# Early gathers of a deformable convolution, staged through three tiles instead of three and then eight

## The chip, the cores and the metric

The kernel runs on one core of one Trainium2 chip. The metric is the device time of one execution in microseconds (us). The time before is the median of 12 runs.

## The reference, cut to what matters

Input `x` is (2, 256, 64, 64) in f32: two images (batches), 256 channels, 64 x 64 pixels. Four layers follow one another:

```
x = attention(x)                  # group norm, 4 heads, 4096 x 4096 scores per head, projection, residual
x = x + position_term             # a linear function of the pixel's place
x = bottleneck(x)                 # 1x1 to 64 channels, deformable 3x3, 1x1 back to 256, residual
h = relu(group_norm(x))           # 32 groups
h = deform_conv(h, dw1, pw1, w1)  # offsets from a 7x7 depthwise and a 1x1 convolution,
h = relu(group_norm(h))           # bilinear samples at 9 taps, 3x3 product
h = deform_conv(h, dw2, pw2, w2)
return h + x
```

A bilinear sample of one pixel and tap needs four neighbours of 256 channels each. The kernel keeps the image in DRAM (`img3`) such that one row of 1024 f32 values holds what a sample needs. A gather fetches 128 such rows, for 128 pixels and one tap: 512 KB. A block of 512 pixels takes 4 x 9 = 36 gathers.

## The kernel before

The kernel is one program written out in Python loops. Its first long stage is `attention`, its second is `deform`. The instructions of the matrix engine (PE), ScalarE (ACT), VectorE (DVE) and GpSimd (POOL) run in the order in which the Python code emits them: line 1666 asks for that with `manual_schedule`. The DMA queue of SyncE (SP) is not in that list. Its order is drawn up by the framework's own planner, and an SP instruction can be moved ahead of others that were emitted earlier. Each queue runs in order once the order is fixed: an instruction that waits holds up all that follow it.

**Attention.** It works through four units (two images, two pairs of heads). A unit is 256 steps `n`, and the main loop (line 677) takes two steps in each turn. Sixteen steps, eight turns, make a block of 256 queries: scores (L580), their maximum (L592), exponentials (L598), transposes (L610) with their copies (L627, L629), and the product with the values (L639). The accumulated product is copied into a tile `o` by DVE (L471), four times in a block. When the block's products are through, the following happens one after another:

- PE transposes the shares of the block, DVE copies them out (`shares`, L504), SP stores them to DRAM (`share_d`, L506) and loads them back spread over the partitions (`f`, L510);
- POOL multiplies `o` by `f` and adds it up (`combine`, lines 514 to 527, in the profile L519, L520, L525). Only then may DVE write the next block's product into `o`, since there is one buffer of `o`, of `f` and of `avs`;
- in every second block SP loads the residual (`res<-xa`, L214), and twelve steps into the block after that PE projects, and SP stores the result (`xa<-res`, L557). There is one buffer of `res` too.

In step numbers counted from a block's start: the shares of the block before are stored at step 0, its `combine` is emitted at step 4, its projection at steps 11 and 12.

**Background work.** Between these steps generators emit work of later layers (line 661). In the last unit these are the bottleneck's first half for image 1, and `early_samples` (line 1234), which the change touches. It computes the offsets for the first two blocks (`EARLY = 2`) of the first deformable convolution on image 0, and gathers their samples while attention still runs. Gathered rows go to DRAM (`samp_d`), since there is no room to keep them, and `deform` reads them back.

**The staging.** One gather goes through one 512 KB tile: POOL issues the indirect DMA from `img3` into the tile (L848), SP issues the store of the tile to `samp_d` (L1278), and then the tile may be gathered into again. `gather` (line 1273) does one store and one gather in each call:

```
if len(stores) > 1 and len(free) < 3 or not gathers and stores:
    dst, four = stores.popleft()
    nc.sync.dma_start(dst, four)
    free.append(four)
if gathers:
    dst, idx = gathers.popleft()
    four = free.popleft()
    self.gather(four, self.img3[0], idx)
    stores.append((dst, four))
```

The main loop makes one call a turn, and two in the turns of steps 10, 12 and 14 (line 726): 11 calls a block. At the start three tiles `xb` are free. When the offsets of the second block have been computed, five tiles that held their inputs join them (`whole`: two `v`, one `k`, two `bx`). From then on eight tiles go round.

A `combine` of POOL stands between the calls of the turn before it and that of its own turn, so 11 gathers lie between one `combine` and the next in POOL's order.

Of the kernel before, what the change touches and what calls it, by code (L numbers as in the profile page):

```python
# [29 lines left out]
EARLY = 2  # L30
# [34 lines left out]
class Net:  # L65
# [1168 lines left out]
    def early_samples(self, bott, pools, held, xp, vp, kp, ps):  # L1234


        nc, a = self.nc, self.a
        T, half = DWK * DWK, DWK // 2
        xs = [vp.tile([P, 8, P], F32, name="v").rearrange("p m c -> p (m c)") for _ in range(2)]
        src = self.xn_d[0].rearrange("(cb p) n -> p cb n", p=P)  # L1240

        def rows(i):
            return max(0, 8 * i - half), min(H, 8 * i + 8 + half)

        def load(i):
            y0, y1 = rows(i)
            for cb in range(2):
                nc.sync.dma_start(xs[cb][:, : (y1 - y0) * W], src[:, cb, y0 * W : y1 * W])


        xbs = [xp.tile([P, 2, 512], F32, name="xb") for _ in range(4)]
        held.append(xbs.pop())
        t = pools["t"].tile([P, 512], F32, name="bst")
        dw = t[:, : 2 * T].rearrange("p (c t) -> p c t", c=2)
        pw = t[:, 2 * T : 2 * T + 4 * K2].rearrange("p (c o) -> p c o", c=2)
        nc.sync.dma_start(dw, a["dw"][0])
        nc.sync.dma_start(pw, a["pw"][0])
        load(0)
        border = kp.tile([P, 2, 512], F32, name="k").rearrange("p u n -> p (u n)")
        wide = border[:, : 8 * (W + DWK - 1)].rearrange("p (r w) -> p r w", w=W + DWK - 1)  # L1260
        nc.gpsimd.memset(wide, 0.0)
        yield True
        wf, whole = [], xs + [border]
        for cb in range(2):
            t = pools["x"].tile([P, 2, 512], F32, name="bx").rearrange("p u n -> p (u n)")
            whole.append(t)
            wf.append(t[:, : T * 2 * K2].rearrange("p (t o) -> p t o", o=2 * K2))
            self.filters(wf[cb], cb, dw, pw)
            yield True
        free = deque(x.rearrange("p u n -> p (u n)") for x in xbs)  # L1270
        gathers, stores = deque(), deque()

        def gather():


            if len(stores) > 1 and len(free) < 3 or not gathers and stores:
                dst, four = stores.popleft()
                nc.sync.dma_start(dst, four)  # L1278
                free.append(four)
# [5 lines that stand above are left out]
            return gathers or stores  # L1285

        self.sample = gather
        for i in range(EARLY):
            idx = bott.corner.tile([P, 4, K2], I32, name="bidx")
            w = bott.corner.tile([P, 4, K2, 4], F32, name="bw4").rearrange("p a k c -> p (a k c)")  # L1290
            w = self.early[i] = w.rearrange("p (s j k t) -> p s j k t", s=2, j=4, t=2)
            steps = self.offsets(
                i, xs,
                lambda s, row: wf[s][:, DWK * row : DWK * row + DWK, :].rearrange(
                    "p t o -> p (t o)"
                ),
                self.vec[:, V_PWB : V_PWB + 1],
                bott.base, idx, None, pools["work"], wide, ps,
                odp=lambda: pools["t"].tile([P, 512], F32, name="bst"), y0=rows(i)[0],
                later=ps.later, w=w,  # L1300
            )
            mine = False
            for done in steps:
                if done == "bank":
                    continue
                while bott.lock and not mine:
                    yield False
                bott.lock = mine = True
                yield True
            bott.lock = False  # L1310
            if i + 1 < EARLY:
                load(i + 1)
            if i + 1 == EARLY:
                free.extend(whole)
            for m in range(4 * K2):
                k, j = divmod(m, 4)
                gathers.append((self.samp_d[i][m * P : m * P + P, :], idx[:, j, k : k + 1]))
# [443 lines left out]
```

## Time and profile before

| | |
|---|---|
| median of 12 runs | 5107.22 us (5102.15 to 5110.67) |
| the profiled execution | 5106.64 us, span 5104.8 us |
| PE busy | 4831.2 us, 95% of the span |
| DVE, ACT, POOL busy | 77%, 64%, 46% |
| DMA of `software_dynamic` (POOL's gathers) | 690.41 MB |
| DMA of `hardware_dynamic` (SP's queue) | 300.73 MB |
| gathers into the staging tiles | 32 into `xb`, 16 into `v`, 16 into `bx`, 8 into `k`: 72 |
| first and last of them, start | 2612.7 us and 2909.5 us |
| stores to `samp_d`, first and last issue | 2616.8 us and 2922.3 us |

A line of the timeline gives the start in us, the time in us, the engine and source line, the operation, the tiles written and read, a count, and in brackets the engine's idle time before it and what ended that. A line of the waits gives the engine and what it was about to do, what it waited for, the total in us, the number of times and the longest. A line of the windows gives, for one stretch, its length and then for each engine the busy us with the number of instructions, the granted PE clock, the busy share of the DMA engines and GB/s. Durations of PE are modelled, since matmuls are pipelined.

### The profile page before, as it was taken

How to read it: one execution, taken by the hardware profiler on the slowest of the kernel's cores; microseconds unless marked ns; L12 is line 12 of the kernel's file. 1: busy time of each engine (PE TensorE's matmuls, PEld its weight loads, DVE VectorE, ACT ScalarE, POOL GpSimd, SP SyncE). 2: the span in 40 equal slices, each digit the busy share in tenths (PEclk: the TensorE clock that was granted, in tenths of full speed). 3: DMA queues.
4: the chain of work that ended last, by engine and by line, in shares of the span. 5: the costliest groups of instructions: out<-in, count | busy, mean ns of one | idle time of the engine just before them, and what ended most of it. 6: DMA issues, size and time to landing. Idle time of an engine off the chain costs nothing. (4 is left out here: it accounts for less than half of the span.)

```text
span 5104.8 us, 101084 instructions
## 1 busy us (share of the span) xinstructions
PE 4831.2 (95%) x38680; PEld 2730.2 (53%) x38680; DVE 3948.4 (77%) x7033; ACT 3283.1 (64%) x5941; POOL 2331.1 (46%) x2256
## 2 busy tenths in 40 slices
PE   8999999999999999999999967779999999999998
PEld 5555565555566555565556534434544544444444
DVE  6878867878768888677667657667788888988888
ACT  5676656666667666666657643347876766666666
POOL 0111111111016777555112347775777676666665
PEclk9999999999999999999999979879999999999999
DMA  5131121111112333332547757669999999999998
GB/s 173 58 100 50 46 70 49 35 47 31 55 53 78 103 100 96 98 89 71 155 139 294 275 212 234 202 225 336 369 356 346 373 378 360 364 397 355 351 357 337
DMA packets 367028, 997.74 MB, mean 195 GB/s; under 512 B 61372, under 2 KB 98810, under 8 KB 366542
## 3 DMA queue, kind: packets, MB, share of 16 engines
q0 software_dynamic: 196560, 690.41, 37.2%
q1 hardware_dynamic: 169438, 300.73, 17.6%
q8 instruction: 304, 4.98, 0.4%
q14 instruction: 182, 1.49, 0.1%
q10 hardware_dynamic: 544, 0.13, 0.0%
HBM read 855.36 MB, written 127.35 MB: 193 GB/s over the span
## 5 line engine op out<-in xcount | busy, mean ns | idle before, releaser
L598 ACT ACTIVATE e<-sc,low 128x1024 f32<-128x1024 f32 x1024 | 1147.4, 1120 | 740.0 <-DVE low L592 737.3
L848 POOL DMA_INDIRECT four<-img,didx x1080 | 1153.6, 1068 | 531.6 <-issue 142.7
L592 DVE TENSOR_REDUCE low<-sc 128x1 f32<-128x1024 f32 x1024 | 1204.4, 1217 | 232.2 <-PE sc L580 227.8
L1545 PE MATMUL out<-st,wc 128*128 128x512 f32 x2304 | 1209.9, 608 | 72.3 <-ACT st L1535 34.0
L580 PE MATMUL sc<-k,qs 64*128 64x512 f32 x2048 | 998.0, 605 | 1.8 <-ACT e L598 1.4
L639 PE MATMUL av<-et,v 128*64 128x256 f32 x8192 | 998.2, 386 | 0.0
L580 PE MATMUL sc<-k,q 64*128 64x512 f32 x2048 | 977.2, 604 | 0.0
L519 POOL TENSOR_TENSOR o<-o,f 128x1024 f32<-128x1024 f32 x63 | 149.6, 2375 | 1766.9 <-DMA f<-share_d 883.8
L610 PEld LDWEIGHTS tt<-ident,e 64*128 64x128 f32 x16384 | 655.2, 139 | 513.0 <-issue 271.1
L629 ACT COPY et<-tt 128x512 f32<-128x512 f32 x1152 | 659.5, 585 | 173.4 <-PE tt L610 172.3
L610 PE MATMUL tt<-ident,e 64*128 64x64 f32 x16384 | 727.4, 226 | 36.1 <-ACT et L629 17.7
L627 DVE COPY et<-tt 128x512 f32<-128x512 f32 x896 | 611.6, 683 | 161.7 <-PE tt L610 161.3
L639 PEld LDWEIGHTS av<-et,v 128*64 128x64 f32 x8192 | 554.0, 137 | 301.7 <-issue 49.1
L848 POOL DMA_INDIRECT bfour<-img,bidx x576 | 587.6, 1020 | 183.9 <-issue 106.7
L1526 PEld LDWEIGHTS pt<-ident,smp 128*128 128x128 f32 x2304 | 328.3, 143 | 621.3 <-issue 479.2
L1495 DVE SCALAR_TENSOR_TENSOR four<-four,dwt 128x512 f32<-128x512 f32 x648 | 484.7, 748 | 220.5 <-ACT four L1489 218.8
L1514 DVE SCALAR_TENSOR_TENSOR smp<-four,dw,smp 128x256 f32<-128x256 f32 x1296 | 625.8, 483 | 33.8 <-ACT smp L1504 1.9
L1489 ACT ACTIVATE four<-four,dwt 128x512 f32<-128x512 f32 x648 | 466.2, 719 | 245.4 <-DMA four<-img,didx 241.6
L1545 PEld LDWEIGHTS out<-st,wc 128*128 128x128 f32 x2304 | 387.3, 194 | 319.3 <-issue 213.5
L580 PEld LDWEIGHTS sc<-k,qs 64*128 64x128 f32 x2048 | 346.3, 188 | 209.6 <-issue 116.5
L1526 PE MATMUL pt<-ident,smp 128*128 128x128 f32 x2304 | 445.1, 276 | 1.6 <-DVE smp L1508 1.1
L805 PE MATMUL pd<-x,wf 128*126 128x512 f32 x840 | 428.5, 592 | 0.0
(194 smaller groups left out, 4857.8 us busy)
## 6 DMA issues: line engine op xcount, KB each, us to landing
f<-share_d SPq DMA_DIRECT2D x128, 256.0 KB
four<-samp_d SPq DMA_DIRECT2D x64, 512.0 KB
xb<-xn SPq DMA_DIRECT2D x55, 512.0 KB
img<-imgt SPq DMA_DIRECT2D x96, 256.0 KB
four<-img,didx POOLq DMA_INDIRECT x1080
xa<-res SPq DMA_DIRECT2D x32, 512.0 KB
samp_d<-xb SPq DMA_DIRECT2D x32, 512.0 KB
xb<-in_x SPq DMA_DIRECT2D x20, 512.0 KB
```

The source lines that it names most:

```text
L580: nc.tensor.matmul(s[:, j, :], lhsT=q[u, i // 2][int(h != j)][halves[j], at : at + P], rhs=k[u][c][halves[j], h, :], start=True, stop=True,)
L592: nc.vector.tensor_reduce(low, s, AX.X, ALU.max, negate=True)
L598: nc.scalar.activation(e.rearrange("p j n -> p (j n)"), s, AF.Exp, bias=blk.low[:, g, c : c + 1], accum_out=blk.sum[:, g, c : c + 1],)
L610: nc.tensor.transpose(pt[:, m, :], e[half, m // 4, m % 4 * P : m % 4 * P + P], self.ident[half, half],)
L627: nc.vector.tensor_copy(dst, pt)
L629: nc.scalar.copy(dst, pt)
L639: nc.tensor.matmul(now["av"][halves[h], :], lhsT=v[u][c][:, m, halves[h]], rhs=ets[j][:, m, h, :], start=(m == 0), stop=(m == 7),)
L848: self.nc.gpsimd.indirect_dma_start(out=dst, out_offset=None, in_=img, in_offset=bass.IndirectOffsetOnAxis(ap=idx, axis=0),)
L1495: nc.vector.scalar_tensor_tensor(uv, four[:, 2 * C :], share(s, 1, 1), uv, ALU.mult, ALU.add)
L1514: nc.vector.scalar_tensor_tensor(smps[s], four[:, c], weight(s, c), smps[s], ALU.mult, ALU.add)
L1526: nc.tensor.transpose(pts[u][:, c, j * P : (j + 1) * P], smp[:, c * P : c * P + P], self.ident,)
L1545: nc.tensor.matmul(outs[ob], lhsT=wc[k][:, c, ob * P : ob * P + P], rhs=sts[u][:, c, :], start=(k == 0 and c == 0), stop=(k == K2 - 1 and ...
```

## The change

The five tiles no longer join. The list `whole` is gone, and so is the condition `len(free) < 3`, which made stores wait while tiles were plenty. Number, size and order of the gathers stay, and so do the 72 stores.

```diff
-        wf, whole = [], xs + [border]
+        wf = []
         for cb in range(2):
             t = pools["x"].tile([P, 2, 512], F32, name="bx").rearrange("p u n -> p (u n)")
-            whole.append(t)
             wf.append(t[:, : T * 2 * K2].rearrange("p (t o) -> p t o", o=2 * K2))
             self.filters(wf[cb], cb, dw, pw)
             yield True
...
-            if len(stores) > 1 and len(free) < 3 or not gathers and stores:
+            if len(stores) > 1 or not gathers and stores:
                 dst, four = stores.popleft()
                 nc.sync.dma_start(dst, four)
                 free.append(four)
...
             if i + 1 < EARLY:
                 load(i + 1)
-            if i + 1 == EARLY:
-                free.extend(whole)
             for m in range(4 * K2):
                 k, j = divmod(m, 4)
                 gathers.append((self.samp_d[i][m * P : m * P + P, :], idx[:, j, k : k + 1]))
```

## The prediction

> **What bounds the kernel now.** The page comes first, for where the time is and where the change acts.
>
> ```profile
> PE 4831.2 (95%) x38680; PEld 2730.2 (53%) x38680; DVE 3948.4 (77%) x7033; ACT 3283.1 (64%) x5941; POOL 2331.1 (46%) x2256
> ```
>
> PE is the bound on average, which says little about the 300 us in which the 72 staged gathers run (2612 to 2922 us). So next comes POOL's timeline over that stretch, which shows three tiles and eight tiles at work, one after the other:
>
> ```profile
> 2606.38 1.26 POOL L520 TENSOR_TENSOR o<-o 128x512 f32<-128x512 f32 x1
> 2607.72 0.72 POOL L525 TENSOR_TENSOR avs<-o 128x256 f32<-128x256 f32 x1
> 2612.65 0.98 POOL L848 DMA_INDIRECT xb<-img,bidx  x1 [4.21 <-DVE bidx L768]
> ...
> 2623.41 0.94 POOL L848 DMA_INDIRECT xb<-img,bidx  x1 [7.27 <-DMA samp_d<-xb]
> ...
> 2633.82 0.94 POOL L848 DMA_INDIRECT xb<-img,bidx  x1 [6.98 <-DMA samp_d<-xb]
> ...
> 2644.77 0.94 POOL L848 DMA_INDIRECT xb<-img,bidx  x1 [6.12 <-DMA samp_d<-xb]
> ...
> 2673.84 0.73 POOL L525 TENSOR_TENSOR avs<-o 128x256 f32<-128x256 f32 x1
> 2674.71 0.97 POOL L848 DMA_INDIRECT v<-img,bidx  x1
> ...
> 2693.00 0.94 POOL L848 DMA_INDIRECT k<-img,bidx  x1 [1.54 <-DMA samp_d<-k]
> 2714.33 2.35 POOL L519 TENSOR_TENSOR o<-o,f 128x1024 f32<-128x1024 f32 x1 [20.39 <-DMA f<-share_d]
> ...
> 2718.12 0.73 POOL L525 TENSOR_TENSOR avs<-o 128x256 f32<-128x256 f32 x1
> ```
>
> The first ten gathers use three `xb`. The 1st, 4th, 7th and 10th start at 2612.65, 2623.41, 2633.82 and 2644.77: a round of three costs 10.4 to 11.0 us, 10.7 on average, and each waits for the store of the tile. From 2674.71 on eight tiles serve, and the 11 gathers between two combines are issued within 18.3 us (to 2693.00). Then POOL idles 20.39 us for `f`. By this view alone the slack is large. SP's timeline of the same block says where `f` is held:
>
> ```profile
> 2702.07 0.32 SPq L1278 DMA_DIRECT2D samp_d<-v  x1
> 2704.55 0.32 SPq L1278 DMA_DIRECT2D samp_d<-k  x1
> 2704.97 0.38 SPq L506 DMA_DIRECT2D share_d<-shares  x1
> 2709.65 1.11 SPq L510 DMA_DIRECT2D f<-share_d  x2
> ```
>
> The store of the 11th gather stands ahead of `share_d` in SP's queue, although the code emits it later: the planner moved it there. `share_d` follows 0.42 us behind it, then `f`, then the combine. Two blocks later the order is the same, and the last store goes out at 2796.00 and `share_d` at 2796.41, while DVE had the shares ready at 2790.68 (2790.41 + 0.27). The waits between 2600 and 2930 us show the next link:
>
> ```profile
> POOL o L519 <- DMA f<-share_d: 107.0, 5, 25.2
> DVE o L471 <- POOL avs L525: 12.2, 5, 5.1
> ```
>
> DVE waits for the combine in five blocks, 5.1 us at the longest. So there is a closed loop: combine, 11 gathers, their stores, `share_d`, `f`, combine. It has no PE in it, and it sets or nearly sets the pace of these blocks. The windows between ends of combines show how near PE is:
>
> ```profile
> 2674.60:2718.90 44.30, 44.16 (x509) 27.48 (x504) 34.85 (x62) 31.64 (x62) 14.73 (x14) 1.00 0.72 274
> 2766.60:2810.10 43.50, 40.92 (x461) 24.82 (x460) 32.23 (x60) 28.34 (x55) 14.70 (x14) 1.00 0.74 279
> ```
>
> PE fills 94% to 100%. Loop and PE are balanced within a few us: whatever is added to the loop is not covered.
>
> **The change part by part.** It adds and removes no instruction and no byte. The condition without `len(free) < 3` does nothing by itself: with three tiles, two outstanding stores leave one free. What acts is that 62 gathers lose five of eight tiles; the first ten had only three before as well.
>
> One full block, from the end of a combine (T0): before, the last store goes out at T0 + 29.98 (2704.55 - 2674.57), + 29.64 and + 29.43 in the next two (2748.49 - 2718.85, 2796.00 - 2766.57): 29.7. After it, by the rows of the first block: the first gather at T0 + 0.1 (2674.71 - 2674.57); the 10th three rounds later, 32.1 us (2644.77 - 2612.65). The 11th follows the 10th as the 5th the 4th or the 8th the 7th, 1.25 or 2.65 us (2624.66 - 2623.41, 2636.47 - 2633.82): I take 2.0. Its store follows by 5.1 us, as that of the 10th did (issue over at 2650.16, so begun at 2649.84), or up to 6.1 as that of the second (2620.02 - 2613.94): 5.4. Sum: 0.1 + 32.1 + 2.0 + 5.4 = 39.6. The loop gets longer by 9.9 us, between 8.7 and 11.2.
>
> Behind it the path is as before: in the block above 9.4 us from `share_d` to the combine's start and 4.5 us of combine. The shares are ready at T0 + 24 to T0 + 30, so `share_d` goes on following the last store. While POOL waits for a tile, only gathers and the next combine are queued behind, and for that one DVE's copy of `o` waits, behind which stand the score maxima, the exponentials, and after a turn PE.
>
> Full blocks with 11 gathers on eight tiles: from 2674.57 to 2901.85 there are five (44.3, 47.7, 43.5, 48.4, 43.4 us). 5 x 9.9 = 49.5 us. The last block has seven gathers (10 + 55 + 7 = 72): its seventh store would go out at T0 + 0.1 + 21.2 + 4.3 = 25.6 instead of 20.4 (2922.30 - 2901.85). But `share_d` waits there for the residual's store and load anyway, until 2933.76. I take 2 of the 5 us. In two of the five blocks `xa<-res` and `res<-xa` stand between the last store and `share_d` (5.7 us, 2748.49 to 2754.16). If the planner now puts them ahead of the last stores, 2 x 4 to 5 us are saved: bounds 39 and 61 with the other terms' ends. I leave them where they are, at + 51.5.
>
> Sum: 5106.6 + 51.5 = 5158. The profiled run is 0.6 us under the median, so against that 5158 or 5159. Nothing is given back later: `deform` starts when attention ends, and its reads of `samp_d` are issued from 2974 us on, 50 us behind the last store.
>
> A rule that speaks against this loss: the Trainium skill, "DMA: Bandwidth & Descriptors", section "Anatomy of one DMA", gives a DMA's time as about 2.0 us and its bytes by 436 GB/s. For 512 KB that is an estimate of 3.2 us, 6.4 us for gather and store, 3 x 6.4 + 1.25 + 3.2 = 24 us for the last landing, earlier than now, and the sum would be nothing. The trace has 4.2 us from gather to store (2612.65 to 2616.84) and 6.6 from store to the next gather (to 2623.41), so the measured round stands.
>
> **The rivals.** *SP's queue gets another order, no change.* SP's order is the planner's. If the slower ring makes it place `share_d` ahead of the last two or three stores, `f` no longer waits for them. Then the 11th gather ends at T0 + 35, and the combine can start when it does now, T0 + 39.8. Cost 0 to 2 us a block: 5107 to 5117, say 5111. For it: 39.6 is later than the shares' 24 to 30. Against it: in the first block with three tiles, ten stores stand ahead of `xa<-res` and `share_d` in SP's order. It decides where `share_d` stands before the ninth store.
>
> *The same order, faster.* If `share_d` goes out as soon as the shares are there, up to 5.7 us earlier, the 12.2 us of DVE's waits could go: down to 5106.6 - 12.2 = 5094. Against it: the combine still has to follow the 11th gather at T0 + 35, and PE has 0.1 to 2.6 us of idle time a block in the windows shown.
>
> *Only PE counts.* In the first block with three tiles (2608 to 2674) the combine waited for DVE's `o`, not for `f`; the ring was hidden by 66 us of PE work. If blocks grow so, less is lost. In the later ones PE has 41 to 47 us, against a loop of 39.6 + 13.9 = 53.5 or more, so half the loss is the most that this may take away: 5118 to 5140.
>
> *More than summed.* Rounds of 12.5 us under the other traffic, or a lower clock after PE's new gaps (1.00 in most of these windows, 0.92 in the last): 5 x 6 us more, about 5190.
>
> **How the numbers follow.** The forecast, 5140 to 5172, gets 0.62; half the loss 0.10; more 0.07: slower 0.79. No change 0.14, faster 0.07. About 0.2% (10 us) is what a measurement of this kernel tells from no change. The range of 8 in 10 takes in the forecast, the half and the edges of its neighbours: 5111 to 5176.
>
> **What would show it.** Right: all 72 gathers into `xb`; POOL waits for `samp_d<-xb` every third gather up to the last; ends of combines 53 to 58 us apart instead of 43 to 48 over five blocks; `share_d` still directly behind the last store or the residual; DVE's wait for `avs` at 40 us or more; PE under 90% between 2675 and 2955. Wrong: `share_d` issued ahead of stores, with combines 44 to 48 us apart (first two rivals), or the distance grown by over 14 us a block (the last).

## The result, and the profile after

The changed kernel takes 5156.06 us (median of 7 runs, 5145.72 to 5160.57); the kernel before, with the runs taken beside it, 5106.58 us. The ratio is 1.0093, with a 95% interval of 1.0084 to 1.0103: 49 us slower, where 51.5 were forecast. In two later comparisons it was 1.0099 (1.0084 to 1.0115) and 1.0103 (1.0087 to 1.0118). The profiled execution has a span of 5152.6 us, 47.8 more than before. Chips differ in speed: the kernel before took 5105 to 5108 us on some ("fast" below), 5285 and 5322 on two others ("slow"), so a ratio is always taken on one chip.

POOL's timeline for the first full block (11 gathers) on three tiles, to be laid beside the eight-tile block of the prediction:

```profile
2673.10 0.73 POOL L525 TENSOR_TENSOR avs<-o 128x256 f32<-128x256 f32 x1
2673.97 0.97 POOL L848 DMA_INDIRECT xb<-img,bidx  x1
...
2684.97 0.94 POOL L848 DMA_INDIRECT xb<-img,bidx  x1 [7.53 <-DMA samp_d<-xb]
...
2696.09 0.94 POOL L848 DMA_INDIRECT xb<-img,bidx  x1 [7.40 <-DMA samp_d<-xb]
...
2707.59 0.94 POOL L848 DMA_INDIRECT xb<-img,bidx  x1 [6.85 <-DMA samp_d<-xb]
2708.91 0.94 POOL L848 DMA_INDIRECT xb<-img,bidx  x1 [0.39 <-issue]
2723.75 2.34 POOL L519 TENSOR_TENSOR o<-o,f 128x1024 f32<-128x1024 f32 x1 [13.90 <-DMA f<-share_d]
```

Rounds of 11.0, 11.1 and 11.5 us, and the 11th gather at T0 + 35.1 (T0 is the end of the combine, 2673.83) instead of + 18.4. POOL still idles for `f` afterwards, 13.90 us. SP's timeline of the same block has the order on which the forecast rested, the last store and then `share_d` right behind it:

```profile
2711.96 2.70 SPq L1277 DMA_DIRECT2D samp_d<-xb  x2
2714.75 0.41 SPq L506 DMA_DIRECT2D share_d<-shares  x1
2718.95 1.11 SPq L510 DMA_DIRECT2D f<-share_d  x2
```

DVE had these shares ready at 2703.66 (T0 + 29.8): `share_d` stood 11 us behind stores. The waits between 2600 and 2980 us:

```profile
POOL xb L848 <- DMA samp_d<-xb: 149.0, 28, 7.8
ACT e L598 <- DVE low L592: 121.6, 49, 13.4
POOL o L519 <- DMA f<-share_d: 72.9, 5, 17.9
DVE o L471 <- POOL avs L525: 54.9, 5, 12.8
```

DVE's wait for the combine goes from 12.2 to 54.9 us in the same five blocks, and it is passed on: ACT's wait for the score maxima is 121.6 us, where it was 79.8 between 2600 and 2930 us before. The windows between ends of combines (first and third full block) show PE, which had filled 94% to 100%, at 86% and 77%, with a granted clock under 1.00:

```profile
2673.80:2728.20 54.40, 46.72 (x534) 28.84 (x530) 34.88 (x62) 33.14 (x64) 14.70 (x15) 0.96 0.66 223
2787.10:2839.40 52.30, 40.45 (x449) 24.68 (x449) 31.87 (x59) 28.42 (x54) 14.68 (x15) 0.89 0.69 232
```

### The profile page after: what moved, and what is told of

Read it like the earlier page. It is cut to its first block, busy times and chain, and to the rows that moved or that the text cites. A ratio compares the mean times of both kernels' runs of the same rounds, so it can differ in the third digit from the quotient of the medians.

```text
span 5152.6 us, 101091 instructions
## 1 busy us (share of the span) xinstructions
PE 4833.7 (94%) x38680; PEld 2728.0 (53%) x38680; DVE 3949.9 (77%) x7033; ACT 3282.9 (64%) x5941; POOL 2327.1 (45%) x2256
## 5 line engine op out<-in xcount | busy, mean ns | idle before, releaser
L639 PEld LDWEIGHTS av<-et,v 128*64 128x64 f32 x8192 | 554.9, 137 | 302.6 <-issue 50.5
```

The source lines that it names most:

```text
L639: nc.tensor.matmul(now["av"][halves[h], :], lhsT=v[u][c][:, m, halves[h]], rhs=ets[j][:, m, h, :], start=(m == 0), stop=(m == 7),)
```

## The experiments

**Fewer or more tiles.** Four tiles, as an edit of the changed kernel:

```diff
             if i + 1 < EARLY:
                 load(i + 1)
+            if i + 1 == EARLY:
+                free.append(xs[0])
```

> One of the five tiles joins again, so four go round. Theory (the loop from combine over the ring, the last store, share_d and f to the next combine; a round costs 10.4 to 11 us): 11 gathers need two waits for a tile instead of three, so the last store goes out about 0.1 + 21.5 + 2.5 to 3.5 + 5.4 = 30 us after the combine, as with eight tiles (29.7). Time 5105 to 5115, ratio 1.000 to 1.002. Rival, each missing tile costs its share (49.5 us over five tiles, four missing): 5140 to 5150. Rival, something else that goes with the change (the two bx and the v and k tiles are free for others earlier): stays at 5150 to 5160.

Ratio 0.9992 (0.9975 to 1.0009), where the kernel before took 5284.59 us. By the time alone my theory held, by the trace it did not: the last store came at T0 + 34.4 to 36.5, not 30, and the five full blocks lasted 255 us, as against 227 before on a fast chip. So I could not tell whether the ring cost nothing or was covered there.

> Four tiles again. On the chip where the kernel before took 5284 us they cost nothing, but there the last store came 34 to 37 us after the combine, not the 30 that I had expected, and the blocks were 48 to 55 us long by themselves. On a chip where the kernel before takes 5106, with 29.7 us for eight tiles and 40 for three: theory, last store at T0 + 35, blocks 5 us longer than before, 25 us in all, ratio 1.004 to 1.006, about half the changed kernel's loss. Rival (my first count, whole rounds only): ratio 1.000 to 1.002. On the slow chip: 0.998 to 1.001 again.

Again a chip of the slow kind (5321.91): 0.9978 (0.9961 to 0.9994). A third run, beside the changed kernel, was on a fast one (5105.1):

> The changed kernel beside four tiles on one chip, whichever it is. Where the kernel before takes about 5106: ratio 1.008 to 1.011, as measured twice. Where it takes about 5300 (blocks of 47 to 55 us even without a ring that holds them): theory, the loop of 50 to 59 us is the same in us, since it has no PE in it, and only what goes beyond the longer blocks is lost: five blocks of 3 to 6 us, ratio 1.002 to 1.006. Rival, the loss is a share of the time: 1.009 there too.

> Four tiles beside the changed kernel. Where the kernel before takes about 5106: last store at T0 + 35 against 30 and 40, so about half the changed kernel's loss, ratio 1.003 to 1.006; rival (whole rounds only) 1.000 to 1.002. Where it takes about 5300: 0.997 to 1.001, as measured twice.

The changed kernel 1.0103, four tiles 1.0056 (1.0042 to 1.0070). POOL's and SP's timelines of four tiles there, in the first full block (T0 = 2676.18):

```profile
2676.33 0.98 POOL L848 DMA_INDIRECT v<-img,bidx  x1
...
2687.54 0.94 POOL L848 DMA_INDIRECT v<-img,bidx  x1 [6.51 <-DMA samp_d<-v]
...
2699.99 0.93 POOL L848 DMA_INDIRECT v<-img,bidx  x1 [5.31 <-DMA samp_d<-v]
2703.89 0.94 POOL L848 DMA_INDIRECT xb<-img,bidx  x1 [2.97 <-DMA samp_d<-xb]
2705.14 0.94 POOL L848 DMA_INDIRECT xb<-img,bidx  x1 [0.30 <-issue]
```

```profile
2710.02 3.06 SPq L1277 DMA_DIRECT2D samp_d<-xb  x2
2713.18 0.38 SPq L506 DMA_DIRECT2D share_d<-shares  x1
```

Two waits instead of three, as counted, but rounds of 11.2 and 12.5 us instead of 10.7, and the last store at T0 + 36.6 (35.7 on average of five blocks). With the fourth tile about half of the loss goes and half stays: the price of a round was wrong in the first count, the loop was right. The five blocks took 254.0 us here and 255.1 and 254.5 on the two slow chips, so the loop of four tiles is equally long on both kinds, and the blocks of 47 to 55 us that the expectation above puts down to the slow chip are this loop's. That four tiles lose nothing on the slow chips is not explained: neither the kernel before nor the changed one was profiled there.

Two tiles from the first gather on:

```diff
-        free = deque(x.rearrange("p u n -> p (u n)") for x in xbs)
+        free = deque(x.rearrange("p u n -> p (u n)") for x in xbs[:2])
```

> Two tiles instead of the changed kernel's three, from the first gather on. Theory: 11 gathers wait five times for a tile, so the last store goes out 0.1 + 5 x (9.5 to 10.7) + 5.1 = 53 to 59 us after the combine, 23 to 29 us a block over eight tiles, five blocks; the last block (seven gathers, three waits) 8 to 12 us more, the first 0 to 5. Sum 120 to 155: 5227 to 5262. Rival, transfers are limited by the DMA engines' rate and fewer tiles only spread them: little more than the changed kernel, 5160 to 5190.

Ratio 1.0108 (1.0070 to 1.0147) on the slow chip, 60 us, half of what I had expected. There POOL's timeline has rounds of two:

```profile
2693.85 0.98 POOL L848 DMA_INDIRECT xb<-img,bidx  x1
...
2702.53 0.94 POOL L848 DMA_INDIRECT xb<-img,bidx  x1 [6.46 <-DMA samp_d<-xb]
...
2740.08 0.94 POOL L848 DMA_INDIRECT xb<-img,bidx  x1 [6.82 <-DMA samp_d<-xb]
```

Five rounds take 46.2 us in this first full block, 9.2 each (8.8 on average of five blocks), and the last store comes at T0 + 47.1 to 50.6 (expected 53 to 59). The five blocks take 309 us, 54 more than with four tiles on the same chip, and the profiled spans differ by 51.8. So nearly all of what the loop adds is there at the end. Of the 60 to 95 us that are missing, the shorter rounds make up 37 (five blocks, last store 48.6 instead of 56); the rest is open, as is the four tiles' result on these chips.

**f out of the stores' way.** Three tiles, and `share_d` and `f` of the last unit's blocks from the ninth on (i >= 8) issued by ACT, `share_d` at the end of a turn and `f` at the start of the next:

```diff
...
-                    nc.sync.dma_start(d, t)
...
+                    if self.u + 1 == len(units) and self.i >= 8:
+                        extra[at, 1] = lambda: give(nc.scalar)
+                        extra[at + 2, 0] = lambda: take(nc.scalar)
+                    else:
+                        give(nc.sync)
+                        take(nc.sync)
...
```

Here `give` issues `share_d` on the queue that it is handed, and `take` issues `f`.

> Three tiles as in the changed kernel, but share_d and f of the last unit's blocks from the ninth on are issued on ACT's queue, out of the way of the stores on SP's. Theory (the loss is f waiting behind the stores): the combine now only has to follow the 11th gather, T0 + 36, so the loop is 36 + 4.5 = 41 us, under PE's 41 to 47, and the loss goes: 5100 to 5115, ratio 0.999 to 1.002; DVE's waits for avs fall from 54.9 to under 15 us. Rival, the ring itself holds the blocks through POOL's order (gathers ahead of the combine): 5140 to 5160.

0.9979 (0.9959 to 0.9998) on the slow chip. Beside the changed kernel on a fast one:

> The changed kernel itself once more, beside the kernel before on the same chip as the three runs that follow, since the chip of the last four ran the kernel before in 5284 us where the first took 5106. Theory: the loop of the staged blocks does not depend on PE, PE's own time does. On a chip like the first, ratio 1.008 to 1.010; on one like the second, where four tiles gave blocks of 47.5 to 55.1 us, five blocks of 54 to 58 us against 51 are 20 to 30 us, ratio 1.003 to 1.006. Rival, the loss is in proportion to the whole time: 1.009 on both.

> Three tiles with share_d and f of the late blocks on ACT's queue, now beside the changed kernel itself. Theory: the loss goes, ratio to the kernel before 0.997 to 1.002, below that of the changed kernel by at least half its loss. Rival, the ring holds the blocks in another way: within 0.001 of the changed kernel.

The changed kernel 1.0099, with ACT's queue 1.0035 (1.0022 to 1.0049): two thirds of the loss are gone with three tiles still going round. DVE's wait for the combine is 0.3 us (55.6 beside it). Of the five full blocks the first, third and fifth took 47.5, 44.1 and 45.8 us (55.0, 53.3 and 50.5 in the changed kernel beside it), the second and fourth still 55.4 and 54.2 (59.1 and 56.8). These two are the ones with `xa<-res` and `res<-xa`. The waits (of all engines between 2600 and 2980 us, of ACT between 2600 and 3000), and SP's and ACT's timelines in the second block (T0 = 2721.84), lead to the reason:

```profile
DVE o L471 <- POOL avs L537: 0.3, 1, 0.3
```

```profile
ACT e L610 <- DMA xa<-res: 20.8, 2, 12.6
```

```profile
2761.64 1.59 SPq L1291 DMA_DIRECT2D samp_d<-xb  x2
2763.33 0.42 SPq L569 DMA_DIRECT2D xa<-res  x1
```

```profile
2748.60 0.31 ACTq L509 DMA_DIRECT2D share_d<-shares  x1
...
2765.76 1.77 ACTq L515 DMA_DIRECT2D f<-share_d  x2
2767.63 1.11 ACT L610 ACTIVATE e<-sc,low 128x1024 f32<-128x1024 f32 x1 [12.64 <-DMA xa<-res]
```

`share_d` went out at T0 + 26.8, `f` only at T0 + 43.9. In the trace each DMA names the semaphore that it raises when it is done, and each wait the semaphores that it waits for: the DMAs of SP and ACT take the same eight in turn (101 to 103, 105 to 108, 110), and each DMA waits for the one that used its semaphore before. ACT stood 12.0 us, until 2765.72, on semaphores 108 and 102 for the first half of `f`, and 102 was the eleventh store's, issued at 2762.92. The second half waited for 103, which was that of `xa<-res`, issued at 2763.33. In the fourth block `f` took the eleventh store's semaphore in the same way (108), 2.8 us behind that store. In the third, `f` took semaphores of the fifth and sixth stores and followed `share_d` by 4.3 us. So in two blocks of five `f` was behind the last store again, from another queue, though it needs no data from it. My next run went by the profile's label alone and moved `xa<-res` to ACT too (blocks 7 to 14 of the last unit):

```diff
-                        nc.sync.dma_start(
-                            rows(self.xa_d[b])[:, :, 512 * i : 512 * i + 512], self.res
-                        )
+                        dst, src = rows(self.xa_d[b])[:, :, 512 * i : 512 * i + 512], self.res
+                        if self.u + 1 == len(units) and self.i >= 7 and self.i < 15:
+                            at = self.u * per_unit + 16 * self.i + 28
+                            extra[at, 1] = lambda: nc.scalar.dma_start(dst, src)
+                        else:
+                            nc.sync.dma_start(dst, src)
```

> Three tiles, share_d and f of the late blocks on ACT's queue as before, and the store of the residual, xa<-res, there too. In the run without the latter, every second block had f at T0 + 43 although share_d was out at T0 + 27 to 30: ACT waited 12 us, in the trace until xa<-res, which stood behind the stores on SP, was through. Theory: that was the rest of the loss; the odd blocks go from 54 to 55 us back to 47 to 49, two blocks of 6 to 7 us: ratio 1.000 to 1.002 where the run without had 1.0035. Rival, ACT's waits for the transfers themselves (share_d's landing ahead of the exponentials) cost the rest: 1.003 to 1.005 still.

By its time inconclusive, since it fell on a slow chip: 0.9973 (0.9959 to 0.9987), as 0.9979 without it on another. ACT's longest wait ahead of `f` was 5.5 us (10.1 in the run without it on the other slow chip), and the second and fourth blocks took 51.5 and 53.0 us (54.6 and 54.3 there), not 47 to 49: `f` came 11 us after `share_d` still. The trace shows why: `f` again takes the eleventh store's semaphore (102 and 108), and goes out 3.3 and 3.1 us behind that store. A run in which `f` shares no semaphore with the stores was not made, so how much of the last third this wait costs is not measured.

Eight tiles with the same detour for `f`:

> The kernel before (three and then eight tiles), with share_d and f of the same blocks on ACT's queue. Theory (before, too, f waits up to 5.7 us behind the stores, and DVE 12.2 us in five blocks for the combine): down to 12 us less, 5094 to 5106. Rival, PE alone holds these blocks: 5106, no difference. Rival, ACT's queue now waits for share_d's landing seven times, 2 to 4.5 us each, ahead of the exponentials: 5106 to 5125.

1.0011 (0.9993 to 1.0029) on the slow chip: no difference shown. The last stores are at T0 + 29.0 to 30.6 there, but DVE has the shares only at T0 + 35 to 39 and the five blocks take 250 us, nearly the 255 of four tiles. In this run, then, something other than the stores paced these blocks; whether the chip or the detour through ACT, no run tells.

**Fewer gathers between combines.** Three tiles, nine calls a block:

```diff
-                for _ in range(1 + (n % 16 in (10, 12, 14))):
+                for _ in range(1 + (n % 16 == 12)):
```

> Three tiles as in the changed kernel, but nine calls a block instead of 11 (the double call stays in one turn only), so nine gathers wait for a tile twice instead of three times. Theory: last store at T0 + 32 instead of 40, 2 us over the eight tiles of before, in seven blocks instead of five and a half, and nine stores ahead of the last block's share_d at the end of attention, up to 8 us: together 10 to 25 us over the kernel before on a chip like the first, ratio 1.002 to 1.005, under half the changed kernel's loss. Rival, the loss goes with the number of gathers through three tiles (62 in both): ratio as the changed kernel, 1.008 to 1.010. Rival, a longer staging delays the start of the next stage: above the changed kernel.

1.0054 (1.0040 to 1.0067), about half the changed kernel's loss and a little over the expected range. All 72 gathers go through three tiles in both, so their number is not what counts. Last stores at T0 + 31.9 to 34.6 in five of six blocks; the six blocks together are 18 us longer than before (289.6 against 271.5), and 5 us more pass between the last combine on POOL and the next stage's first instruction, which there stands right behind the last ten gathers on POOL.

**Stores on POOL.** The kernel before, with its eight tiles:

```diff
-                nc.sync.dma_start(dst, four)
+                nc.gpsimd.dma_start(dst, four)
                 free.append(four)
```

> The kernel before (three and then eight tiles) with the 72 staging stores issued by POOL instead of SP, each six calls behind its gather once eight tiles go round, two calls behind it before. Theory: f is never behind the stores, POOL's eleven pairs of store and gather take 24 to 28 us after the combine, under the 39.8 at which it starts; DVE's 12.2 us of waits shrink, 0 to 10 us less than the kernel before, ratio 0.998 to 1.000. Rival, stores and gathers share POOL's one DMA queue and its order, and a store that waits for its gather holds the gathers and the combine behind it: the first ten gathers 4 us each longer and blocks of 50 us and more, ratio above 1.003.

0.9986 (0.9977 to 0.9995): 7 us faster than the kernel before, and the fastest version on a fast chip. SP's timeline in the first full block (T0 = 2680.17) and DVE's wait between 2600 and 2980 us:

```profile
2710.02 0.33 SPq L506 DMA_DIRECT2D share_d<-shares  x1
2713.61 1.10 SPq L510 DMA_DIRECT2D f<-share_d  x2
```

```profile
DVE o L471 <- POOL avs L525: 4.3, 2, 2.3
```

`share_d` goes out as soon as DVE has the shares (2710.00 in this block; T0 + 25.9 to 29.9 in all), DVE's wait for the combine falls from 12.2 to 4.3 us, and the five full blocks take 220.0 us instead of 227.3. So the kernel before was itself held by the loop, by about that much.

The other half of the change, the condition without `len(free) < 3`, was not run by itself with eight tiles. With three or four tiles it cannot act, since two that wait for their store leave fewer than three free; so the runs above differ by their tiles alone.

## Why the prediction was right, point by point

- *The order on SP* was the open question. The planner kept all eleven stores ahead of `share_d` in all five blocks; the two rivals that put it ahead fell. The prediction had evidence for this order, but gave no reason why the planner keeps to it, and the runs give none either.
- *The ring.* Last store at T0 + 40.5, 40.8, 40.4, 39.7 and 38.4, 40.0 on average, forecast 39.6; against 29.8 before (five blocks), 10.1 us a block, forecast 9.9. The estimate from the page on DMA (24 us) is not borne out: a round cost 10.9 us on average in these blocks (single ones 8.5 to 12.7). The page states its fit for the path of POOL's DMAs, and the estimate used it for SP's stores too.
- *The path behind the last store* was taken as unchanged, and that was the term a little off. From last store to end of combine it took 73 us in the five blocks instead of 78: in the third and fifth `f` followed `share_d` after 2.4 us, where before it took 4.3 and 4.1. The five blocks took 272.9 us instead of 227.3, 45.7 more and not 49.5.
- *The last block* was sized at 2 more and lasted 1.7 less (42.5 against 44.2). The loads `bx<-xa` stood between its stores and `xa<-res` before (at 2924.95), and `res<-xa` followed `xa<-res` after 7.4 us; now that `bx` no longer stages gathers, the planner has these loads 275 us earlier, and `res<-xa` follows after 3.7:

```profile
2617.27 32.23 SPq L1277 DMA_DIRECT2D samp_d<-xb  x10
2649.60 1.26 SPq L911 DMA_DIRECT2D bx<-xa  x2
2650.95 0.48 SPq L557 DMA_DIRECT2D xa<-res  x1
```

- *What comes after.* Of the 47.8 us, 44.3 are there when the next stage begins (its first instruction at 3018.0 instead of 2973.7). The remaining 3.5 appear after that; the prediction had nothing for it. From that first instruction to the end the kernel before took 2131.1 us and the changed one 2134.6, and the other profiles on fast chips lie between 2127.4 and 2138.4, so 3.5 us is not clear of the spread. The sum (47.8 against 51.5) agrees because the ring was right; the path behind it and the last block were both a few us too large, and what comes after happened to make up for part of that.
- *PE.* The rival that only PE counts fell: the blocks lasted 50.5 to 58.9 us with PE busy for 40.5 to 50.2 of them. The lower clock after PE's gaps, a condition of the last rival, did come (0.89 to 0.96 in the five blocks, where it had been 1.00 in four and 0.93 in the other), but it added nothing that shows: the five blocks got 45.7 us longer, where 49.5 were forecast. That the loss runs through `f` is shown by moving `share_d` and `f` alone: three tiles, two thirds of the loss gone. Why slow chips hide it is open.

## What to carry to other kernels

A wait on one engine is worth following to the queue in which the released transfer stands: POOL idled 20 us for `f`, and no spare time was in it, since `f` was queued behind the very stores that fewer buffers delay. Draw the loop (who frees the buffer, what is queued behind that), and price a round from the trace, not a buffer: with three tiles the last of 11 stores went out 10 us later than with eight, with four 6 us, and with nine gathers through three tiles 3 us. A store that waits for a transfer does not belong on the queue of a small transfer that others wait for: moving the stores to another queue made even the kernel with eight tiles 7 us faster. And a second queue is a way out only as far as its waits do not lead back: look at which semaphores they name.

## What the runs showed of the hardware that I had not expected

- A round of gather and store (512 KB each) takes longer the more tiles go round: 8.8 us with two (slow chip), 10.9 with three, 12.5 with four (means of five full blocks), so the cost of one gather falls slowly: 4.4, 3.6, 3.1, and 2.5 us with eight (where stores follow each other 2.5 us apart, with 1 MB gathered and stored in that time).
- The Trainium skill ("Trainium Kernel Development and Optimization", Key Constraints) says that issuing DMAs from several engines saves only the sequencer's issue time. Here two small transfers moved from SP to ACT saved 33 us (1.0099 to 1.0035), since an instruction that waits holds all that stand behind it in its queue; and the move was undone in two blocks of five by a completion semaphore that `f` shared with the eleventh store (102 and 108).
